# Three costs and one delay in the plan of a layernorm + RWKV attention + mixture-of-experts kernel

## The chip, the cores and the metric

The kernel runs on one core of a Trainium2 chip. The metric is device time in microseconds; a lower one is better. It is one launch, all in fp32.

## The reference

The input x has 2 sequences of 2048 rows with 256 channels, 4096 rows in all. Both branches work on the same normalised rows, and both are added to x:

```python
xn = _layernorm(x)                      # no scale, no shift, eps 1e-5
# attention: k, v = xn @ key_w.T, xn @ value_w.T; r = sigmoid(xn @ recep_w.T)
def step(carry, kv):                    # a scan over the 2048 rows of a sequence
    aa, bb, pp = carry; kt, vt = kv
    ww = time_first + pp
    p = jnp.maximum(pp, ww)
    e1, e2 = jnp.exp(pp - p), jnp.exp(ww - p)
    wkv_t = (e1 * aa + e2 * vt) / (e1 * bb + e2 + 1e-06)
    ww2 = time_decay + pp
    p2 = jnp.maximum(pp, ww2)
    e1b, e2b = jnp.exp(pp - p2), jnp.exp(ww2 - p2)
    return (e1b * aa + e2b * vt, e1b * bb + e2b, p2), wkv_t
# attention = (r * wkv) @ out_w.T
# experts: scores = softmax(xn @ gate_w.T + gate_b); the top 2 of 8 with their scores as weights
#   expert(t) = (silu(t @ w1e.T + b1e) * (t @ w3e.T + b3e)) @ w2e.T + b2e       (256 inner)
# shared expert: the same form with 512 inner, for every row
out = x + attention(xn) + sum_of_top2(xn) + shared(xn)
```

## The kernel before

**Tiling.** The 4096 rows are eight chunks (0 to 7) of 512 rows, taken in the order 2, 3, 0, 1, 4, 5, 6, 7. A chunk's rows lie in SBUF as four groups of 128 rows. The dense part (shared expert and attention) works chunk by chunk. The experts work on rows sorted by expert: each row is written twice to a DRAM buffer `xs_d`, at the place its expert and rank give it, and read back as 71 tiles of 128 rows with one expert each.

**Stages.** Each stage is a Python generator, a "flow", that emits instructions.
- `norm_flow` (L444) takes one or two groups: statistics on VectorE (L454, L456), 1/sqrt(variance + eps) on GpSimd as an addition and a power (L459, L460), and the normalisation of even groups on VectorE (L466) and of odd ones by a small VectorE step (L470) and ScalarE (L474).
- `turn_flow` (L478) transposes the chunk on TensorE (L487), copies it out on ScalarE (L493), and makes the gate scores: by_e (L502), held (L508), by_t (L512), sc (L515).
- `route_flow` (L528) needs the scores of all eight chunks, and yields each row's two places.
- `scatter_flow` (L649) writes the rows with 64 indirect DMAs (L661), which GpSimd issues: two for each of the 32 groups. Each second one gets a manual dependency on a TensorE product (`keep_pace`, L640): the last that by the plan's clock had ended `PACE` nanoseconds before that scatter's start.
- `attention_flow` (L722), `mix_flow` (L786, with the products wvp and wrp at L796), `hidden_flow` (L843: product p at L856, ScalarE si at L863, VectorE at L866) and `dense_flow` (L908: product po at L924, sum into xb at L936) are the dense part. `base_flow` (L871) loads xb (L876) and adds the output bias to it (L886); `leave_flow` writes a finished part away (L902).
- `rows_flow` (L956) reads two tiles' rows back with four loads (L966), issued by SyncE once all scatters have landed, and transposes them on VectorE (L970). `goes_flow` (L978) reads where eight tiles' rows have to go, called meta here (one load, L985), and turns it into target places with two small VectorE steps (L989, L990).
- `tile_flow` (L993) is one expert tile: ph on TensorE (L1006), h on VectorE (L1019), silu on ScalarE (L1024), sis on VectorE (L1026), the transpose hsp on TensorE (L1032), its copy on ScalarE (L1036), pos on TensorE (L1042), ys on VectorE (L1046), and an indirect DMA from GpSimd (L1051). Chunks 5, 6 and 7 keep part of their dense work to be run between the tiles.

**What sets the order.** Each engine runs its instructions in the order in which they are emitted, and that order is written by a planner (`Plan`, L81 to L171) while the kernel is built. A flow that yields `on(ns, engine, ...)` asks for an engine for that many nanoseconds, and may name rooms (PSUM banks, buffers) that it needs; a yielded number is a delay before the flow goes on, and a yielded event is waited for. The planner always takes the flow that can start first by its own clock, and among flows within 150 ns of it on the same engine the one with the lowest rank. So a number in a yield costs nothing on the chip; it moves where that step and all later ones stand in the engines' orders. It also sets `plan.begun`, from which `keep_pace` picks its product. Flows of the tiles are added to the plan at the end of `scatter_flow`, with ranks from 10 up.

The planner's clock adds a hop when a flow changes its engine (270 ns after TensorE, 110 after VectorE and ScalarE, 150 after GpSimd) and 1280 ns where ScalarE must change its function table. TensorE's steps ask for PSUM banks (8 in all); h, hsp and pos have rooms of their own beside them.

Of the kernel before, what the change touches and what calls it, by code (L numbers as in the profile page):

```python
# [173 lines left out]
def on(ns, engine, *take, table=None, spare=None, rank=None):  # L174
    return ({engine: ns}, table, take, spare, rank)
# [33 lines left out]
NU = 32  # L209
KEEP = 3  # L210

PACE = 4000

BETWEEN = (2, 4)

# [10 lines left out]
def rwkv_moe_kernel(  # L226
# [136 lines left out]
    def land(nbytes, then, *rooms):  # L363


        def flow():
            yield on(nbytes / 370, "Q")
            yield 2000
            for e in then:
                e.set()  # L370
            for r in rooms:
                r.give()

        plan.add(flow(), 0)
# [69 lines left out]
    def norm_flow(c, groups):  # L444

        first, m = groups[0], len(groups)
        of = f"{c}_{first}"
        yield loaded[c, first]
        xt = xn[c][:, first : first + m, :C]
        yield on(460 * m, "DVE", (STATS, 1))  # L450
        stats = two.tile([P, m, 6], F32, tag="stats", name=f"stats_{of}")
        mv = two.tile([P, m, 2], F32, tag="mv", name=f"mv_{of}")
        for n in range(m):
            nc.vector.bn_stats(stats[:, n, :], xt[:, n, :])  # L454
        for n in range(m):
            nc.vector.bn_aggr(mv[:, n, :], stats[:, n, :])  # L456
        rstd = two.tile([P, m], F32, tag="rstd", name=f"rstd_{of}")
        yield on(400, "POOL")
        nc.gpsimd.tensor_scalar(rstd, mv[:, :, 1], EPS, None, ALU.add)  # L459
        nc.gpsimd.tensor_tensor(rstd, rstd, neg_half.to_broadcast([P, m]), ALU.pow)  # L460

        for n, g in enumerate(groups):
            row = xt[:, n, :]
            if g % 2 == 0:
                yield on(345, "DVE")
                nc.vector.tensor_scalar(row, row, mv[:, n, 0:1], rstd[:, n : n + 1], ALU.subtract, ALU.mult)  # L466
            else:
                yield on(170, "DVE")
                shift = two.tile([P, 1], F32, tag="shift", name=f"shift_{c}_{g}")
                nc.vector.scalar_tensor_tensor(  # L470
                    shift, mv[:, n, 0:1], -1.0, rstd[:, n : n + 1], ALU.mult, ALU.mult
                )
                yield on(430, "ACT")
                nc.scalar.activation(row, row, AF.Identity, bias=shift, scale=rstd[:, n : n + 1])  # L474
            normed[c, g].set()
        STATS.give()
# [163 lines left out]
    def keep_pace(step):  # L640

        tc.add_manual_dep(
            getattr(step, "ins", step),
            plan.product(plan.begun - PACE).name,
            mybir.DependencyInfo(mybir.DependencyClass.Sync, mybir.DependencyReason.DATA),
            reason="pace",
        )

    def scatter_flow():  # L649


        yield have["routed"]

        yield 6000
        for side, chunks in (("left", LEFT), ("right", RIGHT)):
            for c in chunks:
                for n in range(NT):
                    g = c * NT + n
                    for w in range(2):
                        yield on(1340, "POOL")  # L660
                        step = nc.gpsimd.indirect_dma_start(  # L661
                            out=xs_views[2 * g + w],
                            out_offset=bass.IndirectOffsetOnAxis(ap=slot[w][:, g : g + 1], axis=0),
                            in_=xn[c][:, n, :],
                            in_offset=None,
                        )
                        if w:
                            keep_pace(step)
                land(0, [scattered[c]])
            early[side].__exit__(None, None, None)  # L670
            if side == "left":
                pool = ctx.enter_context(tc.tile_pool(name="bias", bufs=1, side="left"))
                for name, shape in (("b13", [P, E, 2, I]), ("b2", [P, E, C])):
                    late[name] = pool.tile(shape, F32, tag=name, name=name)
                plan.add(bias_flow(), 0)
            else:
                late["pool3"] = ctx.enter_context(tc.tile_pool(name="late3", bufs=3, side="right"))
                late["poolg"] = ctx.enter_context(tc.tile_pool(name="lateg", bufs=3, side="right"))
        for j in range(TILES):
            plan.add(tile_flow(j), 10 + j / 100)  # L680
        for j in range(0, TILES, 2):
            plan.add(rows_flow(j), 10 + j / 100)
        for j in range(0, TILES, GO):
            plan.add(goes_flow(j), 10 + j / 100)
        plan.add(collect_flow(), 3)
# [15 lines left out]
    def bias_flow():  # L701
        for c in LEFT:
            yield scattered[c]
        yield have["bias_d"]
        for m in range(2):
            yield on(2600, "SP")
            part = bias_d[ts(m, E * NI), :].rearrange("(e i) p -> e (i p)", e=E)
            nc.sync.dma_start(late["b13"][:, :, m, :], part.partition_broadcast(P))
        yield on(2600, "SP")
        nc.sync.dma_start(late["b2"], b_out[:E, :].partition_broadcast(P))  # L710
        land(P * E * 3 * C * 4, [have["bias"]])
# [244 lines left out]
    def rows_flow(j):  # L956


        for c in range(NCH):
            yield scattered[c]  # L960
        n = min(2, TILES - j)
        yield on(1500, "SP", (U, 1), (ROWS, 1))
        t = u([P, n * P // Q, NC * Q], f"xs_{j}")
        of = xs_d[j * P : (j + n) * P, :C].rearrange("(b t) (q i) -> q t b i", t=Q, i=NC * Q)
        for q in range(P // Q):
            nc.sync.dma_start(t[ts(q, Q)], of[q])  # L966
        yield 3000
        yield on(620, "DVE", (U, 1), (XST, 1))
        xT = u([P, n, NC, P], f"xsT_{j}")
        nc.vector.transpose(  # L970
            xT.rearrange("p n k (b t) -> p n b k t", t=Q), t.rearrange("p (n b) (k i) -> p n b k i", n=n, i=Q)
        )
        U.give()
        ROWS.give()
        turned_rows[j] = [xT, n]
        rows_in[j].set()

    def goes_flow(j):  # L978

        for c in range(NCH):  # L980
            yield scattered[c]
        n = min(GO, TILES - j)
        yield on(400, "SP")
        where = xs_d[j * P : (j + n) * P, R_TO:].rearrange("(n p) c -> p n c", p=P)
        nc.sync.dma_start(meta[:, j : j + n, :], where)  # L985
        yield 4000
        yield on(320, "DVE")
        to, top = meta[:, j : j + n, 0], meta[:, j : j + n, 1]
        nc.vector.tensor_tensor(top, top, likes[:, j : j + n], ALU.is_equal)  # L989
        nc.vector.tensor_tensor(goes[:, j : j + n], to, top, ALU.add)  # L990
        gone[j].set()
# [70 lines left out]
    def collect_flow():  # L1062

        yield have["tiles"]
        for c in DONE:
            for n in range(NT):
                g = c * NT + n
                yield on(420, "SP", (Y, 1))
                y = late["poolg"].tile([P, 2, C], F32, tag="y", name=f"y_{g}")
                nc.sync.dma_start(y, ys_d[2 * g * P : 2 * (g + 1) * P, :].rearrange("(p w) c -> p w c", w=2))  # L1070
                plan.add(combine_flow(c, n, y), 4)
# [52 lines left out]
    for i, c in enumerate(ORDER):  # L1124
# [3 lines left out]
        for n in range(NSI):  # L1128
            between = n == 0 and i in BETWEEN
            plan.add(hidden_flow(c, n), 1 + (i + 0.5) / 10 if between else 30 + i + n / 10)  # L1130
    plan.add(route_flow(), 0.5)
    plan.add(scatter_flow(), 0.5)
    plan.add(bias_rows_flow(), 2)
    plan.add(attention_flow(), 20)
# [93 lines left out]
```

## Time and profile before

| what | us |
|---|---|
| median of three runs (488.91 to 489.56) | 488.96 |
| profiled execution | 494.21 |
| its span | 492.1 |
| TensorE busy, 1683 matmuls | 469.0 |
| VectorE busy, 783 instructions | 393.8 |
| ScalarE busy, 332 instructions | 186.7 |
| GpSimd busy, 205 instructions | 168.6 |
| 64 scatters of rows (L661), mean of one | 1.096 |
| granted TensorE clock, mean | 0.999 |

In the profile PE is TensorE, PEld its weight load, DVE is VectorE, ACT is ScalarE, POOL is GpSimd, and SPq is the queue of DMA issues of SyncE. A timeline row reads: start in us from the start of the span, length in us, engine, line of the kernel, operation, output and inputs, shapes, number of instructions that were put together in the row, and in brackets the engine's idle time before the row and what ended it. "Remote" and "another core or an unknown queue" name an event that the profile can't trace back. "Issue" is time in which an engine waited for nothing that the profile shows. In the slices the span is cut in 40 equal parts of 12.3 us, and a digit is the busy share in tenths. The chain of waits follows the last instruction back through what released it. Landing records are the semaphore updates that a DMA makes as its data arrives.

### The profile page before, as it was taken

The numbers are of one execution on the slowest core, as the hardware profiler recorded it, in microseconds if no ns is written. First come the engines' busy times: TensorE is split into PE (matmuls) and PEld (weight loads), VectorE is DVE, ScalarE is ACT, GpSimd is POOL, SyncE is SP. The second block draws the span as 40 slices with busy tenths as digits, with TensorE's granted clock in tenths as the row PEclk, the third lists the DMA queues.
The fourth block names the chain that finished last, engine by engine and source line by source line (L and its number), as shares of the span: only waits on it lengthen the run. The fifth ranks groups of instructions, "written<-read, shape, count | busy, mean of one in ns | idle before, by whom it ended". The sixth has DMA issues, their size and how long they took to land.

```text
span 492.1 us, 6242 instructions
## 1 busy us (share of the span) xinstructions
PE 469.0 (95%) x1683; PEld 277.3 (56%) x1683; DVE 393.8 (80%) x783; ACT 186.7 (38%) x332; POOL 168.6 (34%) x205
## 2 busy tenths in 40 slices
PE   3989999999989699999999999999999999999996
PEld 1545556446656365555655665565555654444885
DVE  5776999886379697999799778998699875977793
ACT  3767311521320158223923286224932268211000
POOL 6540067677766032334232232333133232000000
PEclk9999999999999999999999999999999999999999
DMA  7999998728344677333323342227321220287872
GB/s 212 372 395 401 211 218 308 256 97 314 126 160 150 114 106 193 84 87 77 76 73 77 98 103 63 77 55 209 78 61 45 81 68 2 90 276 252 285 243 94
DMA packets 92097, 77.36 MB, mean 157 GB/s; under 512 B 52989, under 2 KB 79774, under 8 KB 91808
## 3 DMA queue, kind: packets, MB, share of 16 engines
q1 hardware_dynamic: 85584, 60.12, 44.0%
q0 software_dynamic: 6480, 16.85, 9.6%
q8 instruction: 15, 0.25, 0.2%
q14 instruction: 18, 0.15, 0.1%
HBM read 42.31 MB, written 35.54 MB: 158 GB/s over the span
## 4 chain that ended last, share of the span: by engine, by line
PE 70%; DVE 10%; ACT 10%; issue 5%; DMA 2%; another core or an unknown queue 1%; SPq 1%; POOL 1%; DVEq 0%; ACTq 0%; POOLq 0%
PE p L856 20%; PE ph L1006 15%; PE po L924 12%; PE pos L1042 9%; PE wrp L796 5%; PE wvp L796 5%; ACT L1024 3%; ACT L759 3%; PE hsp L1032 2%; DMA ws<-in_w_sh_dram 2%; DVE aa L811 1%; DVE h L1019 1%; ACT sis L1024 1%; PE tp L487 1%
## 5 line engine op out<-in xcount | busy, mean ns | idle before, releaser
L1051 POOL DMA_INDIRECT ys_d<-ys,goes x71 | 78.3, 1103 | 186.5 <-DVE ys L1046 164.4
L1006 PE MATMUL ph<-we,xsT 128*128 x284 | 133.1, 593 | 2.8 <-issue 2.8
L856 PE MATMUL p<-xnT,ws 128*128 128x512 f32 x256 | 114.0, 593 | 0.3 <-DMA ws<-in_w_sh_dram 0.3
L661 POOL DMA_INDIRECT xs_d<-xn,slot x64 | 70.1, 1096 | 53.8 <-DMA we<-in_w_exp_dram 27.8
L856 PEld LDWEIGHTS p<-xnT,ws 128*128 128x128 f32 x256 | 47.8, 190 | 54.9 <-issue 52.4
L1006 PEld LDWEIGHTS ph<-we,xsT 128*128 128x128 f32 x284 | 50.1, 190 | 40.4 <-issue 39.1
L1042 PEld LDWEIGHTS pos<-we,hsT 128*128 128x128 f32 x284 | 53.5, 190 | 31.3 <-issue 19.8
L1042 PE MATMUL pos<-we,hsT 128*128 x284 | 70.2, 381 | 0.8 <-ACT hsT L1036 0.8
L924 PE MATMUL po<-ws,si 128*128 128x256 f32 x256 | 59.7, 380 | 1.6 <-issue 1.0
L1019 DVE TENSOR_TENSOR h<-ph,b 128x512 f32<-128x512 f32 x71 | 48.6, 686 | 14.2 <-PE ph L1006 12.4
L1024 ACT ACTIVATE sis<-h 128x256 f32<-128x256 f32 x71 | 29.0, 415 | 71.5 <-DVE h L1019 70.4
L924 PEld LDWEIGHTS po<-ws,si 128*128 128x128 f32 x256 | 48.5, 190 | 12.9 <-issue 5.4
L863 ACT ACTIVATE si<-p,vec 128x512 f32<-128x512 f32 x32 | 21.5, 684 | 63.2 <-PE p L856 55.7
L1036 ACT COPY hsT<-hsp 128x256 f32<-128x256 f32 x71 | 24.4, 368 | 47.1 <-PE hsp L1032 34.9
L1026 DVE TENSOR_TENSOR sis<-sis,h 128x256 f32<-128x256 f32 x71 | 29.1, 414 | 11.0 <-ACT sis L1024 10.2
L1046 DVE TENSOR_TENSOR ys<-pos,b 128x256 f32<-128x256 f32 x71 | 28.6, 414 | 8.1 <-PE pos L1042 5.3
L924 PE MATMUL po<-wo,rw 128*128 128x256 f32 x128 | 32.4, 379 | 1.5 <-issue 1.4
L824 ACT ACTIVATE th<-wrp 128x512 f32<-128x512 f32 x16 | 9.6, 598 | 59.0 <-PE wrp L796 45.5
L796 PE MATMUL wrp<-xnT,wr 128*128 128x512 f32 x64 | 30.1, 592 | 0.0
L796 PE MATMUL wvp<-xnT,wv 128*128 128x512 f32 x64 | 29.0, 593 | 0.0
L924 PEld LDWEIGHTS po<-wo,rw 128*128 128x128 f32 x128 | 24.3, 190 | 7.9 <-issue 4.7
L1032 PEld LDWEIGHTS hsp<-ident,sis 128*128 128x128 f32 x142 | 18.2, 141 | 17.3 <-issue 9.2
(128 smaller groups left out, 531.8 us busy)
## 6 DMA issues: line engine op xcount, KB each, us to landing
xs<-xs_d SPq DMA_DIRECT2D x140, 64.0 KB
xs_d<-none SPq DMA_DIRECT2D x17, 516.0 KB
y<-ys_d SPq DMA_DIRECT2D x32, 256.0 KB
xb<-in_x_dram SPq DMA_DIRECT2D x8, 512.0 KB
we<-in_w_exp_dram SPq DMA_DIRECT2D x16, 256.0 KB
pa<-part_d SPq DMA_DIRECT2D x8, 512.0 KB
xn<-in_x_dram SPq DMA_DIRECT2D x14, 256.0 KB
part_d<-xb SPq DMA_DIRECT2D x5, 512.0 KB
```

What stands on the lines that cost most here:

```text
L661: step = nc.gpsimd.indirect_dma_start(out=xs_views[2 * g + w], out_offset=bass.IndirectOffsetOnAxis(ap=slot[w][:, g : g + 1], axis=0), in_ ...
L796: nc.tensor.matmul(pt, wa[name][:, k, ts(ch, P)], xnT[c][k], start=(k == 0), stop=(k == NC - 1))
L856: nc.tensor.matmul(pt, ws13[:, m, k, ts(i, P)], xnT[c][k], start=(k == 0), stop=(k == NC - 1))
L924: nc.tensor.matmul(po[:, j, :], l[:, ts(2 * half + j, P)], r, start=(i == 0), stop=(i == len(parts) - 1))
L1006: nc.tensor.matmul(ph, xT[:, k, :], we[:, bass.ds(ev, 1), 0:2, k, :], start=(k == 0), stop=(k == NC - 1))
L1019: nc.vector.tensor_tensor(h, ph, late["b13"][:, bass.ds(ev, 1), :, :], ALU.add)
L1024: nc.scalar.activation(si, h[:, 0, :], AF.Silu)
L1026: nc.vector.tensor_tensor(si, si, h[:, 1, :], ALU.mult)
L1032: nc.tensor.transpose(tp[:, i, :], si[:, ts(i, P)], ident)
L1042: nc.tensor.matmul(po, hT[:, i, :], we[:, bass.ds(ev, 1), 2, i, :], start=(i == 0), stop=(i == NI - 1))
L1046: nc.vector.tensor_tensor(y, po, late["b2"][:, bass.ds(ev, 1), :], ALU.add)
L1051: nc.gpsimd.indirect_dma_start(out=ys_views[j], out_offset=bass.IndirectOffsetOnAxis(ap=goes[:, j : j + 1], axis=0), in_=y, in_offset=None ...
```

## The change

Four numbers of the plan change. The GpSimd step of the norm is counted at 950 ns plus 150 ns for each group, instead of 400 ns. A row scatter is counted at 1290 ns instead of 1340. The product on which each second scatter waits is looked up 2000 ns before that scatter's planned start instead of 4000. After the last scatter, `scatter_flow` lets 5000 ns of planned time pass before it adds the flows of the tiles, of their rows and of their places. No instruction is added or removed by the flows themselves; their order changes on all engines, and with it where ScalarE's table loads fall.

```diff
-PACE = 4000
+PACE = 2000
@@ norm_flow
         rstd = two.tile([P, m], F32, tag="rstd", name=f"rstd_{of}")
-        yield on(400, "POOL")
+        yield on(950 + 150 * m, "POOL")
         nc.gpsimd.tensor_scalar(rstd, mv[:, :, 1], EPS, None, ALU.add)
@@ scatter_flow
                     for w in range(2):
-                        yield on(1340, "POOL")
+                        yield on(1290, "POOL")
                         step = nc.gpsimd.indirect_dma_start(
@@ scatter_flow
                 late["poolg"] = ctx.enter_context(tc.tile_pool(name="lateg", bufs=3, side="right"))
+
+        yield 5000
         for j in range(TILES):
             plan.add(tile_flow(j), 10 + j / 100)
         for j in range(0, TILES, 2):
             plan.add(rows_flow(j), 10 + j / 100)
         for j in range(0, TILES, GO):
             plan.add(goes_flow(j), 10 + j / 100)
```

Lines after the last hunk are two higher in the changed kernel than in the one before.

## The prediction

> **What bounds the kernel now.** I read the busy times and slices first, then the chain of waits, then the gaps of TensorE one after the other, and at each gap the timelines of the engines that feed it.
>
> ```profile
> PE 469.0 (95%) x1683; PEld 277.3 (56%) x1683; DVE 393.8 (80%) x783; ACT 186.7 (38%) x332; POOL 168.6 (34%) x205
> ...
> PE   3989999999989699999999999999999999999996
> ...
> PE 70%; DVE 10%; ACT 10%; issue 5%; DMA 2%; another core or an unknown queue 1%; SPq 1%; POOL 1%; DVEq 0%; ACTq 0%; POOLq 0%
> ```
>
> TensorE is the bound: 469.0 of 492.1 us. Its slices of 12.3 us dip in the first, in slices 3, 12 and 14 (25 to 37, 135 to 148 and 160 to 172 us), and in the last. The change removes no matmul, so it can move only the idle time of TensorE. In the TensorE timeline the pauses over 0.15 us add to 20.3 us: 8.0 before 30 us, 3.3 at 133.5 to 138.2, 2.9 at 162.6, 1.3 at 170.7, and under 0.8 each elsewhere. After 187 us it hardly pauses, so what the start of the expert tiles loses or gains there reaches the end unchanged. The profiled execution took 494.21 us (492.1 of span, 2.1 around it), 5.25 over the median of 488.96. The pause at 133.5 to 138.2 hangs in the chain on "another core or an unknown queue" (5.96 us at 132.42), on which POOL and DVE wait too. I read it as a disturbance of the profiled execution. All sums are differences, put on the median.
>
> **Part 1: the norm step counted at 950+150m (1,250 for two groups) where it was 400.** No instruction changes, only places. TensorE before, at its pause near 25 us:
>
> ```profile
> 26.35 0.41 PE L487 MATMUL tp<-ident,xn 128*128 128x128 f32 x2 [0.87 <-issue]
> 27.15 0.66 PE L487 MATMUL tp<-ident,xn 128*128 128x128 f32 x4 [0.39 <-ACT xn L474]
> ...
> 28.46 1.98 PE L856 MATMUL p<-xnT,ws 128*128 128x512 f32 x4
> ```
>
> It waits for the last rows of chunk 5; VectorE and GpSimd, before:
>
> ```profile
> 28.36 0.22 POOL L459 TENSOR_SCALAR rstd<-mv 128x2 f32<-128x2 f32 x1 [1.56 <-DVE mv L456]
> 28.67 0.71 POOL L460 TENSOR_TENSOR rstd<-rstd,neg_half 128x2 f32<-128x2 f32 x1
> ...
> 29.41 0.41 DVE L466 TENSOR_SCALAR xn<-xn,mv,rstd 128x256 f32<-128x256 f32 x1 [0.35 <-POOL rstd L460]
> ```
>
> The POOL pair lasts 0.22+0.71, about 1.0 with its start, so 1,250 is nearer to it than 400. The later count makes the plan put the next group's statistics (L454, 0.72 a pair) before the normalisation that waits for rstd, and, on TensorE, put a ready product of the shared expert (L856, the 1.98 us row) ahead of chunk 5's transposes, where TensorE now waits 1.04, 0.56 and 0.61 (2.21). Placing the rows anew with these durations, the last by_t (L512), which starts the routing, comes at 41.7 where it was 44.02, a gain of 2.3; 0.2 may go to shared-expert products that then stand close behind their inputs. I take 2.1; the ends are 1.2 (only the 1.04 covered, little else) and 2.4. x lands in time for both orders (chunk 7 at 21.4, used after 30).
>
> **Part 2: pace 2,000 and scatters at 1,290.** Each second of the 64 scatters (L661) waits for the product that the plan had ended 2 us, before 4 us, ahead of it. Following every such wait, in the changed order each names the same product or an earlier one: shorter scatters stand earlier in the plan, by more than the 2 us that the pace gives back. POOL before:
>
> ```profile
> 65.66 1.17 POOL L661 DMA_INDIRECT xs_d<-xn,slot  x1 [2.73 <-PE po L924]
> ...
> 89.12 0.96 POOL L661 DMA_INDIRECT xs_d<-xn,slot  x1 [1.59 <-PE p L856]
> ...
> 131.34 0.95 POOL L661 DMA_INDIRECT xs_d<-xn,slot  x1 [1.13 <-PE po L924]
> ...
> 138.64 0.96 POOL L661 DMA_INDIRECT xs_d<-xn,slot  x1 [2.56 <-remote]
> ...
> 156.64 1.22 POOL L661 DMA_INDIRECT xs_d<-xn,slot  x1 [0.30 <-issue]
> ```
>
> The unavoidable 0.3 taken off, the waits at 89.12, 131.34 and 138.64 are 1.29, 0.83 and 2.26. The second at 65.66 stays, as it moves with TensorE. The last lies in the disturbance, so of 4.4 us I count 1.29+0.83 = 2.1 as won, with ends of 0 and 4.4. Between the waits a scatter takes (157.86−65.66−4.4)/63 = 1.39 us; its count in the plan changes nothing of that.
>
> **Part 3: tiles laid 5 us later.** SyncE and VectorE at the start of the tiles, before:
>
> ```profile
> 157.40 0.37 SPq L876 DMA_DIRECT2D xb<-in_x_dram  x1
> 160.98 1.82 SPq L966 DMA_DIRECT2D xs<-xs_d  x4
> 162.84 0.65 SPq L985 DMA_DIRECT2D meta<-xs_d  x1
> 163.60 3.97 SPq L966 DMA_DIRECT2D xs<-xs_d  x8
> 167.62 0.45 SPq L985 DMA_DIRECT2D meta<-xs_d  x1
> ```
>
> ```profile
> 168.89 0.68 DVE L1019 TENSOR_TENSOR h<-ph,b 128x512 f32<-128x512 f32 x1
> ...
> 171.35 0.42 DVE L1026 TENSOR_TENSOR sis<-sis,h 128x256 f32<-128x256 f32 x1
> ...
> 173.21 0.15 DVE L989 TENSOR_TENSOR meta<-meta,likes 128x8 f32<-128x8 f32 x1
> ```
>
> (a) The 512 KB load of xb for chunk 4 (157.40) goes behind the first xs loads and all nine meta loads. It ran beside the last scatter, which by the landing records landed 2.5 us after its end (157.86 to 160.35) where earlier ones took 1.1. xs waits for it. Gain 1.4, ends 0 and 1.4. The load's own users (L886, 1.22; L936, 0.65) move from VectorE's idle 161 to 166 us into a stretch where it is 88 to 90% busy; ph_9 and ph_10 wait for the two banks they free. That stands inside (c).
>
> (b) The destination rows: VectorE takes its instructions in order, and the second and third meta (L989, L990) now stand in front of h_0 and h_1 (L1019), where before they came after sis. By the landing records they landed 9.24 and 11.84 us after xs_0's issue at 160.98. With 0.36 for the pair, h_0 comes at +9.6 where it was 168.89−160.98 = +7.9; then L744, the third meta at +12.2, L747 (0.74), h_1 (0.68), sis_0 at +13.6, and the first hsp, for which TensorE waits, at +14.0; before it was 171.87−160.98 = +10.9. Loss 3.1 relative to xs_0's issue. Behind these waits stand h, sis and xsT, so ScalarE's silu and TensorE's hsp and pos. Nothing covers it: ph_0 to ph_2 are 5.4 us of matmuls and end at +9.7 (+12.5 where TensorE comes late).
>
> (c) ScalarE then has eight instead of six table loads in tiles 5 to 10.
>
> ```profile
> 182.37 1.28 ACT L759 ACT_TABLE_LOAD   x1
> 183.67 0.63 ACT L759 ACTIVATE e1b<-e1b 128x512 f32<-128x512 f32 x1
> 184.31 1.28 ACT L1024 ACT_TABLE_LOAD   x1
> ```
>
> Each is 1.28 us, and the next operation starts 0.02 after it; two are 2.6 of ScalarE. Placed by hand with VectorE's moved L886 and L936, TensorE stalls about 0.8 at pos_5 (ends 0 and 1.3).[...]
>
> (d) At the last tiles two table loads go, and with them TensorE's pauses of 0.53 and 0.44 at 389.6 and 410.9: −0.5, ends 0 and −1.0.
>
> **The sum.** xs_0's issue comes earlier by 2.1 (routing) + 2.1 (pace) + 1.4 (landing) = 5.6. From there to the end it costs 3.1+0.8 = 3.9 more, and 0.5 less at the last tiles. Net −5.6+3.9−0.5 = −2.2: 488.96−2.2 = 486.8 (the profiled execution near 492.0 if its disturbance recurs). TensorE is then at ph_0 near 160.2, 2.4 earlier than its 162.57; xs_0's issue at 155.4 and +4.3 to ph_0 gives 159.7, so neither side adds a wait there. The change pays only if xs_0's issue comes more than 3.9−0.5 = 3.4 us earlier.
>
> **Rivals.** *All of the pace waits are real*, also without the profiler: xs_0 is 7.9 earlier, net −4.5: 484.4. For it: the records of 138.64. Against it: the excess of 5.25 over the median.
>
> *The change doesn't do what it says*: the scatters aren't held by the pace where it counts, in unprofiled runs TensorE is ahead of it and the waits don't exist. Then xs_0 gains 2.1+1.4 = 3.5, net −0.1: 488.9. For it: of the 63 steps from one scatter to the next, 59 show only the 0.3 us of the issue.
>
> *Slower*: the two meta waits in front of h_0 and h_1 decide. If xs_0's issue gains only the routing's 2.1 (the last scatter lands 2.5 late anyway[...]), the price is 3.9−0.5−2.1 = +1.3: 490.3, with the table loads at their upper end 490.8. It decides below 3.4 us of gain. For it: the metas' landings are measured and their order is fixed[...].
>
> **How the numbers follow.** The likeliest 0.36 (own range 485.3 to 488.0, by the ends of parts 1 to 3), all waits real 0.15 (484.4), no pace effect 0.21 (488.9), slower 0.28 (490.3). What a measurement of this kernel can tell from no change is 0.2%, 0.98 us: under 487.98 is faster, over 489.94 slower. So 0.50 faster, 0.22 the same, 0.28 slower. The range reaches from a little under the second case, 484.0, to the slower one, 490.4; about 2 in 10 lie outside, most above.
>
> **What would show it.** Part 1: no pause at 25 to 28 us, last by_t near 41.7. Part 2: first scatters near 63.5 and no waits for PE at the 17th, 47th and 51st. Part 3: xs_0's issue near 155.4; VectorE idle in front of L989 on a meta's landing; a pause over 1 us before the first hsp; eight table loads in tiles 5 to 10; none of the pauses near 390 and 411. The prediction is wrong if xs_0's issue moves by under 3.4 us, if metas land much earlier than +9.2, or if a disturbance like that at 133 us turns out to be the kernel's own.

## The result and the profile after

The changed kernel takes 493.47 us (493.28 to 493.70), the kernel before 488.94 beside it: ratio 1.0093, interval 1.0076 to 1.0111. It is 4.5 us slower, where the forecast was 2.2 faster and its range ended at 490.4. The experiments were run at five sittings, each on another chip; at three of them (the runs again to old_norm, after_again to early_meta, before_move and part_move) executions of every kernel differ among themselves by some us and the kernel before has a median of 492 to 493, so each ratio is taken to the kernel before at the same sitting.

The profile of before that the prediction was read from turned out to hold things that the program does not do each time. A third profile of the same kernel, before_third, has a span of 486.87 and fits the median; it is the one to compare with. From its page, the busy times, the slices of TensorE and the granted clock:

```profile
PE 469.1 (96%) x1683; PEld 278.1 (57%) x1683; DVE 393.9 (81%) x783; ACT 186.9 (38%) x332; POOL 170.5 (35%) x205
...
PE   3999999999999799999999999999999999999996
...
PEclk9999999999999999999999999999999999999999
```

The same lines of the changed kernel:

```profile
PE 471.5 (96%) x1683; PEld 279.3 (57%) x1683; DVE 392.2 (80%) x783; ACT 186.8 (38%) x332; POOL 168.8 (34%) x205
...
PE   3999999999998799999999999999999999999996
...
PEclk9999999999999799999999999999999999999999
```

TensorE is 2.4 us busier with the same 1683 matmuls, and the clock row has a 7 in the slice from 160 to 172 us. There its timeline reads, before (third profile):

```profile
160.91 5.39 PE L1006 MATMUL ph<-we,xsT 128*128 x12 [2.86 <-issue]
166.75 0.41 PE L1032 MATMUL hsp<-ident,sis 128*128 128x128 f32 x2 [0.45 <-issue]
```

and after:

```profile
162.23 8.16 PE L1008 MATMUL ph<-we,xsT 128*128 x12 [3.81 <-issue]
171.44 0.41 PE L1034 MATMUL hsp<-ident,sis 128*128 128x128 f32 x2 [1.05 <-issue]
```

The first hsp is 4.69 us later, and that is the whole loss: from it to the end of the span both take the same, 320.12 and 320.10. VectorE between the first tile's rows and sis, before (third profile):

```profile
163.78 0.68 DVE L1019 TENSOR_TENSOR h<-ph,b 128x512 f32<-128x512 f32 x1
...
165.63 0.69 DVE L1019 TENSOR_TENSOR h<-ph,b 128x512 f32<-128x512 f32 x1
166.23 0.42 DVE L1026 TENSOR_TENSOR sis<-sis,h 128x256 f32<-128x256 f32 x1
...
168.10 0.16 DVE L989 TENSOR_TENSOR meta<-meta,likes 128x8 f32<-128x8 f32 x1
```

after:

```profile
166.36 0.17 DVE L991 TENSOR_TENSOR meta<-meta,likes 128x8 f32<-128x8 f32 x1 [0.79 <-DMA meta<-xs_d]
...
167.08 0.69 DVE L1021 TENSOR_TENSOR h<-ph,b 128x512 f32<-128x512 f32 x1 [0.35 <-issue]
...
169.38 0.17 DVE L991 TENSOR_TENSOR meta<-meta,likes 128x8 f32<-128x8 f32 x1 [1.00 <-DMA meta<-xs_d]
...
170.32 0.68 DVE L1021 TENSOR_TENSOR h<-ph,b 128x512 f32<-128x512 f32 x1
170.93 0.41 DVE L1028 TENSOR_TENSOR sis<-sis,h 128x256 f32<-128x256 f32 x1
```

The two waits for meta, 0.79 and 1.00, stand in front of h_0 and h_1, as the prediction had placed them: the four matmuls of ph_0 end at 165.98, and h_0, behind the second meta, starts at 167.08. SyncE issues the first xs load, before (third profile) and then after:

```profile
156.36 1.82 SPq L966 DMA_DIRECT2D xs<-xs_d  x4
```

```profile
157.44 1.82 SPq L968 DMA_DIRECT2D xs<-xs_d  x4
```

It was to come 5.6 us earlier and comes 1.1 later. The account, all in us, "before" by the third profile:

| point | before | after | difference | predicted |
|---|---|---|---|---|
| last by_t starts | 43.79 | 44.16 | +0.37 | −2.1 |
| first scatter | 61.49 | 60.50 | −0.99 | −2.1 |
| second scatter | 65.44 | 65.81 | +0.37 | −2.1 |
| last scatter ends | 154.20 | 155.84 | +1.64 | −4.2 |
| first xs issue | 156.36 | 157.44 | +1.08 | −5.6 |
| first hsp, after that issue | 10.39 | 14.00 | +3.61 | +3.1 |
| end, after the first hsp | 320.12 | 320.10 | −0.02 | +0.3 |
| span | 486.87 | 491.54 | +4.67 | −2.2 |

Each column is one execution. The two differ in when TensorE reached its full rate (16.09 and 17.63 us; in the changed kernel the four passes of p take 3.57 at 14.41 and 1.88 at 19.52), and that moves the first rows; "The clock" below takes this apart.

### The profile page after: what moved, and what is told of

Same layout as the page of the kernel before. It is cut to its first block, busy times and chain, and to the rows that moved or that the text cites. A ratio compares the mean times of both kernels' runs of the same rounds, so it can differ in the third digit from the quotient of the medians.

```text
span 491.5 us, 6226 instructions
## 1 busy us (share of the span) xinstructions
PE 471.5 (96%) x1683; PEld 279.3 (57%) x1683; DVE 392.2 (80%) x783; ACT 186.8 (38%) x332; POOL 168.8 (34%) x205
## 4 chain that ended last, share of the span: by engine, by line
PE 76%; DVE 9%; ACT 7%; issue 3%; DMA 2%; SPq 1%; DVEq 1%; ACTq 0%
PE p L858 23%; PE po L926 15%; PE ph L1008 15%; PE pos L1044 9%; PE wrp L798 5%; PE wvp L798 5%; PE hsp L1034 2%; ACT L1026 2%; ACT L761 2%; DVE h L1021 2%; DMA ws<-in_w_sh_dram 2%; PE tp L487 1%; DVE aa L813 1%; DVE ys L1048 1%; DVE xsT L972 1%
## 5 line engine op out<-in xcount | busy, mean ns | idle before, releaser
L1053 POOL DMA_INDIRECT ys_d<-ys,goes x71 | 76.5, 1077 | 187.3 <-DVE ys L1048 165.5
L1008 PE MATMUL ph<-we,xsT 128*128 x284 | 136.1, 604 | 3.8 <-issue 3.8
L858 PE MATMUL p<-xnT,ws 128*128 128x512 f32 x256 | 115.5, 601 | 0.1
L661 POOL DMA_INDIRECT xs_d<-xn,slot x64 | 72.3, 1130 | 48.8 <-DMA we<-in_w_exp_dram 25.8
L1008 PEld LDWEIGHTS ph<-we,xsT 128*128 128x128 f32 x284 | 51.2, 194 | 42.2 <-issue 40.9
L972 DVE STREAM_TRANSPOSE xsT<-xs 128x512 f32<-128x512 f32 (+1 forms) x36 | 25.0, 694 | 10.1 <-DMA xs<-xs_d 9.5
L868 DVE SCALAR_TENSOR_TENSOR si<-p,vec,si 128x512 f32<-128x512 f32 x32 | 23.5, 744 | 6.6 <-PE p L858 4.0
```

Of the source, the lines that this page charges most:

```text
L661: step = nc.gpsimd.indirect_dma_start(out=xs_views[2 * g + w], out_offset=bass.IndirectOffsetOnAxis(ap=slot[w][:, g : g + 1], axis=0), in_ ...
L858: nc.tensor.matmul(pt, ws13[:, m, k, ts(i, P)], xnT[c][k], start=(k == 0), stop=(k == NC - 1))
L972: nc.vector.transpose(xT.rearrange("p n k (b t) -> p n b k t", t=Q), t.rearrange("p (n b) (k i) -> p n b k i", n=n, i=Q))
L1008: nc.tensor.matmul(ph, xT[:, k, :], we[:, bass.ds(ev, 1), 0:2, k, :], start=(k == 0), stop=(k == NC - 1))
L1053: nc.gpsimd.indirect_dma_start(out=ys_views[j], out_offset=bass.IndirectOffsetOnAxis(ap=goes[:, j : j + 1], axis=0), in_=y, in_offset=None ...
```

## Experiments

### One part at a time, and the kernel before again

again is the kernel before, unchanged. norm_only, pace_1290 and old_norm put parts of the change in or take them out:

```diff
# norm_only, on the kernel before          # old_norm is the changed kernel with the reverse
-        yield on(400, "POOL")
+        yield on(950 + 150 * m, "POOL")
# pace_1290, on the kernel before
-PACE = 4000
+PACE = 2000
-                        yield on(1340, "POOL")
+                        yield on(1290, "POOL")
```

> The kernel before, unchanged, profiled a second time. If the pause of TensorE at 133.5 to 138.2 us and the 2.56 us of GpSimd at 138.64 were a disturbance of the first profile, both are gone and the span is near 486.9 (488.94 less the 2.1 around a span), so 5.2 shorter; if they are the kernel's own, they are there again at the same place, and the span is near 492. Theory of the tile start (waits for meta[...]): ph_0 comes after a pause of under 3 us, at the full rate (5.4 us for its 12 matmuls), near 160 us.

Measured: 494.20, span 492.2. VectorE, ScalarE and GpSimd in that profile, each at its wait for TensorE:

```profile
137.52 0.69 DVE L936 TENSOR_TENSOR xb<-po,xb 128x512 f32<-128x512 f32 x1 [9.27 <-PE po L924]
```

```profile
137.58 0.69 ACT L863 ACTIVATE si<-p,vec 128x512 f32<-128x512 f32 x1 [4.61 <-PE po L924]
```

```profile
137.77 0.96 POOL L661 DMA_INDIRECT xs_d<-xn,slot  x1 [2.34 <-PE po L924]
```

The first is the sum that in before_third waits to 130.52:

```profile
130.52 0.69 DVE L936 TENSOR_TENSOR xb<-po,xb 128x512 f32<-128x512 f32 x1 [2.27 <-PE po L924]
```

Three engines are released within 0.25 us, VectorE 7 us after TensorE's own records show the product done. I read it as signals of TensorE that come late. VectorE is then behind, and TensorE pauses 3.35 us at 150.7 for a si of VectorE (L866). So the expectation failed in both its forms: the pause was neither gone nor at its old place. Only its last part held (ph_0 after a pause of 2.35, its 12 matmuls in 5.39). Such late signals stand between 86 and 160 us in the first profile of before and in all ten profiles of the three sittings with the higher medians; in the other nine profiles, before_third and the changed kernel's first among them, there is none of it.

> The kernel before with only the norm step counted at 950+150m. The order on VectorE and TensorE before 45 us is that of the changed kernel, and the second meta stands in front of h_0 (the third behind h_1). Theory A, the start of the tiles loses the time (meta waits of VectorE[...]): 491.5 to 493.5, with at least 8 us for the first 12 ph matmuls. Theory B, the norms' new order loses it before 45 us: last by_t 1 us or more later than in the kernel before, and 491 to 493. Theory C, the pace: as before, 488.9.

> The kernel before with only the pace at 2000 and the scatters at 1290. The order before 45 us is that of before; second and third meta both stand in front of h_0. Theory A: 491.5 to 494, VectorE waits for both metas before h_0. Theory B: 488.9. Theory C, the pace lets scatters collide with other work: scatters mean over 1.12 us and 491 to 493.

> The changed kernel with the norm step counted at 400 again. Before 45 us it is ordered as before; at the tiles, the load of xb for chunk 4 stands ahead of the first xs again and the second and third meta behind h_2, as in the kernel before. Theory A: 488.5 to 489.5, as before. Theory B: the same. Theory C: 491 to 493, as the pace and the scatters are those of the changed kernel.

Measured against the kernel before at the same sitting: norm_only 1.0029 (0.9990 to 1.0068), pace_1290 1.0114 (1.0091 to 1.0137), old_norm 1.0065 (1.0041 to 1.0090). norm_only could not be told from no change. Its middle lies under what theories A and B named, but its interval reaches their lower ends (1.0052 and 1.0042); in its profile the first 12 ph matmuls took 5.39 and not 8. old_norm was to be as before by theory A and is 3 us slower: A alone does not suffice. In its profile the first xs issue came at 159.71, 3.35 later than in before_third, and the first hsp 12.45 after it, with no meta in front of h_0 and h_1; TensorE had paused 6.20 us and then took 8.12 for its first 12 matmuls at half clock. The middle of pace_1290 lies above the ranges of all theories, and its mean scatter of 1.091 is not over the 1.12 of theory C. Its profile shows a pause of TensorE of 9.04 at 152.3 behind late signals, after which the meta waits lay in TensorE's shadow (ph_0 at 171.01, hsp at 176.16), so the time says nothing on them.

The second scatter tells more. Before (third profile), in norm_only, in pace_1290 and in the changed kernel:

```profile
65.44 1.18 POOL L661 DMA_INDIRECT xs_d<-xn,slot  x1 [2.73 <-PE po L924]
```

```profile
63.47 1.54 POOL L661 DMA_INDIRECT xs_d<-xn,slot  x1 [2.36 <-PE po L924]
```

```profile
68.72 1.05 POOL L661 DMA_INDIRECT xs_d<-xn,slot  x1 [4.45 <-PE p L856]
```

```profile
65.81 1.38 POOL L661 DMA_INDIRECT xs_d<-xn,slot  x1 [4.10 <-DVE bb L775]
```

With the pace at 4000 it waits for the last product po, with 2000 for the product p behind it. (The row of the changed kernel names a step of VectorE that ended at 65.63, shortly after that p.) Counted from the last by_t, the second scatter stands at 19.93 in norm_only, at 21.65 in before_third and in the changed kernel, and at 23.37 in pace_1290 and old_norm. Each step is 1.72, as long as one product p takes (42.44 to 44.16 in the changed kernel). So the new norm order leaves one product less between the routing and this scatter, and the pace of 2000 adds one: the two cancel. The first scatter, which waits for no product, does come sooner by the new norm order, 16.34 after the last by_t where it was 17.70.

### The meta waits

after_again is the changed kernel, unchanged. The others move VectorE's meta steps alone; all other instructions keep their order.

```diff
# late_meta (late_all: every j but 0, two each behind h_2, h_4, h_6, h_8)
         yield on(320, "DVE")
-        to, top = meta[:, j : j + n, 0], meta[:, j : j + n, 1]
-        nc.vector.tensor_tensor(top, top, likes[:, j : j + n], ALU.is_equal)
-        nc.vector.tensor_tensor(goes[:, j : j + n], to, top, ALU.add)
+        if j in (GO, 2 * GO):
+            put_off.append(places)      # places() holds the three lines above
+        else:
+            places()
         gone[j].set()
@@ tile_flow, after h
+        if j == 2:
+            for places in put_off:
+                places()
# early_meta, on the kernel before: the places of j = 8 and 16 are emitted ahead of h_0 and h_1
```

> The changed kernel, unchanged, a second time, so that it stands beside the experiments on one chip. If the loss is in the order (theory A, meta waits and the pause at the start of the tiles), the ratio to the kernel before is again 1.006 to 1.011, the first hsp again 14.0 us after the first xs issue, and TensorE's clock is again at half for some time[...]. If it was chance of the first runs (theory D: pauses that fall differently in each run), the ratio is within 0.997 to 1.004.

> The changed kernel with the second and third meta step of VectorE moved behind h_2, nothing else. Theory A, part 1 (meta waits): first hsp at +11 after the first xs issue if TensorE runs at full rate, at +12.5 to +13.2 if the clock is halved; 1.0 to 3.1 us faster than the changed kernel. Theory D: no difference to it.

> The kernel before with the second meta step of VectorE moved ahead of h_0 and the third ahead of h_1, as the changed kernel has them, nothing else. Theory A: first hsp at +14 instead of +10.9 after the first xs issue, and 3 us slower than the kernel before (ratio 1.006). Theory B or C or D: no slower.

> The changed kernel with all meta steps but the first put off: second and third behind h_2, two more behind h_4, h_6 and h_8. The pause of 1.3 us at the second tile that was left in late_meta is gone, so by theory A first hsp at +11 after the first xs issue and 2.5 to 3.1 us faster than the changed kernel, ratio to the kernel before 1.003 to 1.005. If the meta waits were only a part that other waits cover: as late_meta, 1.007.

| run | ratio to before | interval | first hsp after first xs issue |
|---|---|---|---|
| after_again | 1.0109 | 1.0077 to 1.0141 | 13.64 |
| late_meta | 1.0070 | 1.0044 to 1.0095 | 11.21 |
| early_meta | 1.0048 | 1.0023 to 1.0073 | 13.15 |
| late_all | 1.0042 | 1.0027 to 1.0056 | 12.66 |

The loss stays with the order (theory D falls). The half clock did not come again at the tiles in after_again: TensorE was late there, had a pause of 1.64 in front of ph_0 and ran at the full rate, so its +13.64 is made by the meta waits without the clock. The meta steps alone, put ahead of h_0 and h_1 in the kernel before, cost 0.48%, 2.4 us (in its profile 3.4 us at half clock are part of that). Taken away from the changed kernel they give 1.9 in late_meta, where the fourth meta, waited for behind h_2, left a pause of 1.32 at the second tile, and 2.5 in late_all. The intervals of late_meta and after_again overlap a little, and late_all is set against the changed kernel's 1.0093 at another sitting; the three together are theory A in size. late_all did not reach +11, since the halved clock now shows:

```profile
162.00 8.28 PE L1017 MATMUL ph<-we,xsT 128*128 x12 [3.55 <-issue]
170.11 0.38 PE L1046 MATMUL hsp<-ident,sis 128*128 128x128 f32 x2
```

Nothing is idle in front of hsp any more; TensorE itself ends ph_2 late.

### The clock

```diff
# late_fill: late_meta, and in tile_flow for j == 0 ahead of the ph products
+            for _ in range(4):
+                nc.tensor.matmul(ph.rearrange("p m i -> p (m i)"), ident, ws13[:, 0, 0, :], start=True, stop=True)
# warm_before, warm_after: in turn_flow for the first chunk ahead of its transposes
+                for _ in range(8):
+                    nc.tensor.matmul(tp[0][:, :P], ident, ident, start=True, stop=True)
```

> As late_meta, with four extra products of 128x512 on TensorE (about 3.4 us at full rate, results overwritten) in its pause before ph_0. Theory A, part 2 (the clock): no half rate after the pause, ph_0 to ph_2 in 5.4 us, first hsp at +11, and 1 to 2 us faster than late_meta; together about 3 us faster than the changed kernel, so 490 to 490.6 where that has 493.5. If the halved clock costs nothing because VectorE sets the pace there: as late_meta.

Measured: 1.0058 (1.0037 to 1.0078) against 1.0070 for late_meta, not told apart. In its profile late signals had made TensorE late (free at 167.4), and the filler pushed ph_0 from there to 170.85: with no pause to run in it cost its whole 3.43. What the clock costs is not tested by it.

The executions of late_all say more. Nine of its 13 had a mean granted clock of 0.991 or 0.992 and took 490.89 to 492.68; of the four at 0.996 to 0.999 three took 488.80 to 489.57, about as the kernel before, and one 491.23. The four of the changed kernel all had 0.992 or 0.993.

> The kernel before with eight products of 128x128 (identity by identity, overwritten) on TensorE from about 2 us, while it waits for x. Theory G (TensorE reaches its full rate[...] at 13.3 to 16.4 us): full rate before 8 us, last by_t 0.5 to 1.5 us earlier, 0.5 to 1.5 us faster. If the prelude is held by VectorE and the loads alone: no difference.

> The changed kernel with the same eight products. Theory G: it loses more by the late full rate (17.6 us), so the last by_t comes 1.5 to 2.2 us earlier, near 42.2, and it is 1 to 2 us faster. If not the clock but VectorE's wait for chunk 0's rows holds the prelude: last by_t within 0.5 of 44.16.

Measured: warm_before 1.0003 (0.9992 to 1.0014), warm_after 1.0056 (1.0037 to 1.0074), which is 1.8 us less than the changed kernel's 1.0093 at its own sitting. In warm_before full rate came at 6.23, was lost from 9.6 to 13.0, and the last by_t stood at 43.68, 0.11 earlier: TensorE does not hold the prelude there; that VectorE's norms do is my reading. In warm_after, where the products start at 1.58, full rate came at 4.82 and was halved again from 8.2 to 15.0; still the last by_t stood at 42.43, 1.73 earlier than in the changed kernel, and the first xs issue 1.20 earlier. In the changed order TensorE, which from 13.9 to 44 us does not pause at all, has become the bound of the prelude, and each us at half rate counts.

That goes for executions without the products too, and when the full rate comes differs from execution to execution: the same instructions up to the last by_t had it at 16.29 in after_again and at 17.63 in the changed kernel's first profile. These are all profiles without added products:

| norm order | full rate from | last by_t |
|---|---|---|
| new (no_scan, after_again, late_meta, norm_only) | 15.50, 16.29, 16.56, 17.00 | 42.62, 43.22, 43.41, 43.54 |
| new (changed, late_all, late_fill) | 17.63, 17.63, 19.22 | 44.16, 44.19, 44.85 |
| old (before, again, before_third, old_norm, early_meta) | 13.28, 13.66, 16.09, 16.11, 16.41 | 44.02, 43.79, 43.79, 43.74, 43.86 |
| old (before_move, pace_1290) | 18.80, 19.15 | 45.31, 45.35 |
| new but for the first three chunks (norm_part, part_late) | 16.01, 16.02 | 43.17, 43.16 |

At a like time of the full rate the new order brings the last by_t some 0.6 earlier (43.22 against 43.79). Part of warm_after's 1.73 may then be this chance as well: its full rate came for good at 15.06, little before that of no_scan.

### The prelude and the scatters

```diff
# norm_part, on the changed kernel (part_late: with late_all; warm_part: with the eight products too)
-        yield on(950 + 150 * m, "POOL")
+        yield on(400 if c in ORDER[:3] else 950 + 150 * m, "POOL")
# no_scan, on the changed kernel; aa and bb
-        nc.vector.tensor_tensor_scan(aa[:, 1:], e1b, uu, aa[:, 0:1], ALU.mult, ALU.add)
+        nc.vector.tensor_tensor(aa[:, 1:], e1b, uu, ALU.mult)
```

> The changed kernel with the norm step counted at 400 for the first three chunks only. VectorE and TensorE begin as in the kernel before, the later part is that of the changed kernel. Theory E (in the changed kernel VectorE waits for chunk 0's rows with chunk 3's normalisations queued behind, and TensorE comes to its full rate later, which eats part 1's gain): last by_t near 42, 1.4 to 2 us ahead of the changed kernel's, and about as much faster in all where nothing else gives it back. Rival: the prelude's order does not reach the end, as the scatters are held by TensorE's products: last by_t earlier, total as the changed kernel.

Measured: 1.0084 (1.0071 to 1.0097). The last by_t came at 43.17, 0.99 earlier than in the changed kernel's profile and not 2, the first xs issue 1.03 earlier; but the total moved by some 0.4, less than can be told. And the 0.99 is not shown to be the order's: by the table above, the whole new order has 43.22 at a like time of the full rate. What was given back in this profile is seen at the tiles:

```profile
160.81 5.39 PE L1008 MATMUL ph<-we,xsT 128*128 x12 [3.38 <-issue]
170.34 0.66 PE L1034 MATMUL hsp<-ident,sis 128*128 128x128 f32 x2 [4.13 <-issue]
170.79 3.00 PE L1008 MATMUL ph<-we,xsT 128*128 x4
```

TensorE came earlier, ran ph_0 to ph_2 at full rate, waited 4.13 for the meta chain, and ran the next tile at half rate (3.00 for the 4 matmuls that take 1.88).

The wait that theory E names is there in the changed kernel's prelude, VectorE and then TensorE:

```profile
10.50 0.75 DVE L454 BATCH_NORM_STATS2 stats<-xn 128x6 f32<-128x256 f32 x2 [1.62 <-DMA xn<-in_x_dram]
```

```profile
14.41 3.57 PE L858 MATMUL p<-xnT,ws 128*128 128x512 f32 x4
```

The statistics of chunk 0 wait 1.62 for its rows, and chunk 3's normalisation stands behind them. The four passes of p take 3.57 at half rate; in the first profile of before they took 1.98, in before_third 3.03. But in after_again, with the same order and a wait of 1.32 at that place, they take 3.01: that the order makes the full rate come later is not shown.

> norm_part and late_all together, a try at a kernel that is no slower than the one before. If both effects add: 4 to 5 us faster than the changed kernel, ratio to the kernel before 0.998 to 1.002. What is then left over 1.000 is the scatters, which last longer in the changed order.

> part_late with the same eight products. Theory G: 0.5 to 1.2 us faster than part_late, ratio to the kernel before 0.999 to 1.001, or under that where both clock losses vanish.

Measured: part_late 1.0018 (1.0004 to 1.0031), warm_part 1.0017 (1.0004 to 1.0030). part_late is 3.7 us under the changed kernel, at another sitting, a little short of the 4 to 5; at its own sitting it is 1.2 under late_all. In its profile the clock was not halved, though the pause in front of ph_0 is longer than late_all's 3.55:

```profile
161.14 5.39 PE L1017 MATMUL ph<-we,xsT 128*128 x12 [3.72 <-issue]
167.66 0.41 PE L1046 MATMUL hsp<-ident,sis 128*128 128x128 f32 x2 [1.12 <-issue]
```

Four of its 14 executions had a mean granted clock of 0.992 or less, where late_all had nine of 13. Whether the norm order or chance makes that difference is not shown. The eight products added nothing to it: last by_t 0.68 earlier, first xs issue 0.61 earlier, and then a half-rate stretch of 3.4 us at the tiles.

> The changed kernel with VectorE's two scans of the attention (aa and bb, 1.28 us each) replaced by one product of the same operands (0.68 us), so the attention's recurrence is left out. Theory F (a scatter takes longer than 0.96 us where a scan of VectorE runs beside it): the mean of a scatter falls from 1.13 to under 1.06 us and the steps from one to the next from 1.43 to under 1.36. If the excess comes from the transfers instead: unchanged, 1.13.

Two scatters of the changed kernel, and VectorE at the same time:

```profile
139.88 1.61 POOL L661 DMA_INDIRECT xs_d<-xn,slot  x1 [0.30 <-DMA xs_d<-xn,slot]
141.79 1.87 POOL L661 DMA_INDIRECT xs_d<-xn,slot  x1 [0.30 <-issue]
143.96 0.96 POOL L661 DMA_INDIRECT xs_d<-xn,slot  x1 [0.30 <-issue]
```

```profile
139.44 1.28 DVE L738 TENSOR_TENSOR_SCAN pp<-tdp,pp,zero 128x512 f32<-128x512 f32 x1
...
141.60 1.28 DVE L813 TENSOR_TENSOR_SCAN aa<-e1b,aa,uu 128x512 f32<-128x512 f32 x1
```

These two, which start while a scan runs, take 1.6 and 1.9 us and the free one 0.96. Of the 63 scatters after the first, 11 start so in this profile; they take 1.01 to 1.87. The group of all 64, in the changed kernel:

```profile
L661 POOL DMA_INDIRECT xs_d<-xn,slot x64 | 72.3, 1130 | 48.8 <-DMA we<-in_w_exp_dram 25.8
```

in no_scan:

```profile
L661 POOL DMA_INDIRECT xs_d<-xn,slot x64 | 68.5, 1070 | 48.8 <-DMA we<-in_w_exp_dram 25.8
```

Its one execution took 489.86. The mean falls to 1.07, the step to 1.368: the direction of theory F, a little short of its numbers, as the scan of pp is still there and scatters without a scan beside them lengthened, from 3.4 to 4.8 us in all. Of the changed kernel's excess over 0.96 (10.6 us in all after the first scatter) 7.3 lie on the 18 scatters with a scan beside them, in no_scan 2.0 of 6.8 on 5; in before_third it is 6.5 of 9.4, on 20. So in the changed order not more of them meet, but those that do take longer, 0.41 over the 0.96 each where it was 0.33.

> The kernel before, a third profile. If undisturbed, its span is near 487; with 320.1 from the first hsp to the end as in all other profiles, the first hsp is at 166.8 and, at +10.9 or +11.2, the first xs issue near 155.7, against 157.44 in the changed kernel. Then 1.7 of the 4.5 us arise before the tiles. Theory F (scatters beside scans): steps from scatter to scatter of 1.39 us again, against 1.43.

Measured: 489.52 at 1.0003 (0.9989 to 1.0017), span 486.87, first hsp at 166.75 as foreseen, the first xs issue at 156.36 where 155.7 was worked out. Between its second and last scatter there is no wait for TensorE at all. The step is 1.409, not 1.39.

### A version that beats the kernel before

```diff
# before_move: kernel before with late_all's meta order; part_move: warm_part. Both, in hidden_flow:
-        if c in LAST:
+        if (c, i) in ((LAST[0], 0),):
+            yield scattered[ORDER[-1]]
+        elif c in LAST:
             yield turn[TILES - 5]
```

> The kernel before with the first hidden product pair of chunk 5 (two products, 1.7 us each) asked for at the time of the last scatter, where it was asked for at the last tiles, and all meta steps of VectorE but the first put off behind h_2, h_4, h_6 and h_8. If TensorE's pause before ph_0 (2.9 us) is what it could have worked in: p0_5_0 runs in the pause, 1.5 to 2.9 us faster than the kernel before, ratio 0.994 to 0.997. If the order of VectorE or the buffers held by the early result give it back: 0.999 to 1.004.

> warm_part with the same product pair of chunk 5 asked for at the time of the last scatter. The pause of 3.6 us before ph_0 becomes 1.9, no half rate after it, and the work is gone from the end: 2 to 3 us faster than warm_part, ratio to the kernel before 0.995 to 0.998. Otherwise as for before_move.

Measured: before_move 0.9991 (0.9980 to 1.0003), part_move 0.9974 (0.9955 to 0.9992). The first is no gain that can be told. part_move is 1.3 us faster than the kernel before; against warm_part, at another sitting, the ratios 1.0017 and 0.9974 make it 2.1 us faster, at the lower end of what was expected. Its profile does not show the expected pause of 1.9: late signals had made TensorE late, and it paused 0.40 in front of ph_0. No half rate followed. One of the moved products runs between the ph products of the first two tiles:

```profile
165.53 1.88 PE L863 MATMUL p<-xnT,ws 128*128 128x512 f32 x4
```

and from the first hsp to the end there are 319.05 us left in place of 320.1.

## Why the prediction was wrong

**The bound** was read rightly: nothing after the first hsp changed, and the loss is idle (and slow) time of TensorE before it.

**The sum.** xs_0's issue was to come 5.6 earlier and came 1.08 later. Of the 6.7 us between, 2.5 are part 1, 2.1 the pace waits of part 2, 1.3 the steps between scatters and 0.8 the landing of part 3 (a). From there to the end only 0.2 are missed.

**Part 1** ("I take 2.1; the ends are 1.2 ... and 2.4") failed: the last by_t came 0.37 later. The pauses near 25 us that were to be filled belong to an execution in which TensorE had its full rate from 13.28 us. In before_third the rate comes at 16.09, the pauses are 0.23 at most, and the last by_t is no later (43.79): they were slack. In the changed order TensorE works without a pause from 13.9 to 44, and so the last by_t moves with the time of the full rate, which the prediction put at nothing. At a like time the new order gains 0.6; in the profile of the table the later rate (17.63) takes more than that. The sentence "x lands in time for both orders" looked at the last chunks only; it fails for chunk 0, though no run shows that this wait costs anything at the last by_t.

**Part 2** ("I count 1.29+0.83 = 2.1 as won") failed in three places. The waits at 89.12 and 131.34 are as little the program's own as the one at 138.64 that I left out; before_third has none, and so there was nothing to win. This was the rival that the change doesn't do what it says. And "in the changed order each names the same product or an earlier one" does not hold at the second scatter: with the pace of 2000 it waits for p where it waited for po, 1.72 us later, which takes back what the new norm order gains there. That the scatter's count "changes nothing" of the 1.39 us a step was wrong in effect: the order moved, scatters beside scans took longer, and 63 steps grew by 0.020 each, 1.3 us.

**Part 3 (a)**, 1.4 for the last scatter's landing, was 0.56 (2.16 to 1.60 from its end to the xs issue): in an undisturbed execution the load of xb for chunk 4 is issued at 150.06, 4.1 us before the end of the scatters, and so there was less to gain. In the first profile, with the load beside the last scatter, the issue came 3.12 after that end; the last landing record stands at 160.84 there, and not at the 160.35 that the prediction read.

**Part 3 (b)**, the meta waits, was right to the digit: hsp at +14.0 and it is at +14.00. The loss is 3.6 and not 3.1, because the kernel before does it in 10.39 when nothing disturbs it. early_meta and late_all show it in the time, 2.4 and 2.5 us, so about half of the whole loss.

**Part 3 (c) and (d)**: eight table loads in place of six are there between 165 and 215 us, and a pause of 0.52 in front of the pos products at 188.1; of the pauses near 390 and 411 the second went and the first grew (0.89 at 389.3). Net nothing, −0.02 where 0.3 was forecast. In the changed kernel, too, each of the eight takes 1.28, and ScalarE's next operation starts 0.01 to 0.02 after it (180.19 and 181.49 for the first).

**What was left out** is the clock. The prediction saw no wait of TensorE at ph_0 (160.2 against 159.7) and counted all of its work at full rate. In the changed kernel's trace the granted clock is 0.50 for 6.8 us from 161.0, beginning within a pause of 3.81 that ends at 162.23. In that trace it costs nothing more at the tiles, as h waits for meta anyway; with meta out of the way the first hsp comes 1.4 later with it than without (+12.66 in late_all, +11.23 in part_late), and in norm_part's profile it returned what was gained before.

The rival that came nearest is the slower one, in its mechanism and its break-even: under 3.4 us of gain at the first xs issue the change loses. It, too, kept part 1's 2.1, and so ended 3.2 us short.

## What to carry to other kernels

Before a pause is booked as a gain, look whether it is the program's or that execution's: what lies between the profiled execution's time and the median has to be taken out of every row, not only of the one that looks odd. When a planner moves small steps that wait for a DMA ahead of other work in an engine's order, their landing time becomes that work's start: here VectorE took up the metas at 166.36 and 169.38, and h_0 and h_1 at 167.08 and 170.32. Where TensorE pauses for as long as it did here (3.28 us and more), count the next few us of its work at half rate as a case of its own: in these profiles it came after 11 of 14 such pauses. And before two profiles are set against each other, compare when TensorE reached its full rate in each: in three profiles of one program it was 13.28, 13.66 and 16.09.

## What the runs showed of the hardware

- TensorE's full rate began between 13.3 and 19.2 us in 16 profiles without added products at the start, with first work at 5.5 to 6.1, in the same program at 13.28, 13.66 and 16.09. In the changed kernel it began at 17.63: the 16 matmuls of by_e take 1.10 at 9.89 and 0.65 at 17.91. Later, in all 20 profiles together, the rate fell to half for 3.4, 6.8 or 10.2 us at a time. It did so at all six pauses of 4.0 us and more (4.00 in early_meta, 4.13 in norm_part, 6.20 in old_norm and 9.04 in pace_1290 among them), and at 3.28 (before_move), 3.35 (again), 3.55 (late_all), 3.57 (warm_part) and 3.81 (after), but not at 3.38 (norm_part), 3.67 (after_again) and 3.72 (part_late). Single pauses of 2.2 to 2.9 (2.35 in again, 2.76 in before, 2.86 in before_third) were not followed by it, but in norm_only two of 1.65 and 2.65 within 10 us were, and in late_meta, late_fill and after_again a row of pauses of 1.2 and less. So the length of a pause alone does not decide.
- A scatter that GpSimd issues took 0.96 us at its shortest, and up to 1.87 with a scan of VectorE beside it. With two of the scans replaced (no_scan) the mean of the 64 fell from 1.130 to 1.070. What makes a scatter take longer beside a scan is not shown.
- Between 86 and 160 us some steps that wait for TensorE's products start late in some executions: the same sum into xb starts at 137.52 in again and at 130.52 in before_third, another at 132.99 in part_move and at 123.00 in part_late. I read that as signals of TensorE that come late, by 7 and by 10 us. In at least five of these eleven profiles TensorE itself also stutters: in late_meta it starts single matmuls 1.41 us apart from 133.12 to 140.16, and the clock is at half from 136.03. Why was not found; it happens in both kernels, in every profile of three sittings and in none of the other two.
- Left open: what the new norm order would bring with the pace at 4000 and the meta steps put off. The second scatter 1.72 earlier in norm_only, counted from the last by_t, speaks for it; it was not run. Left open too is how much of the 4.5 us the half clock makes by itself, as no run took it alone away.
